# First linear-attention stage of a twelve-stage transformer kernel: every engine in the written order, attention between the other half's feed-forward products, elu without GpSimd, norms in two parts

## The chip, the core and the metric

The kernel runs on one core of a Trainium2 chip. The core has a matrix engine (TensorE, PE in the profile; its weight loads are PEld), VectorE (DVE), ScalarE (ACT), GpSimd (POOL) and a queue engine that issues transfers (SyncE, SP). Each works through its own queue in order and waits on semaphores for the others. Matrix products land in PSUM and have to be copied out ("evacuated") by VectorE or ScalarE before their buffer is free again. The metric is device time in microseconds, the median over several executions; one execution is also recorded by the profiler.

## The reference, cut to what matters

Twelve stages work one after another on a token array of 16 x 64 tokens with 256 features. The change concerns the second, `l0_attn`: four encoder layers with linear attention over blocks of 64 tokens, and a final norm.

```python
qp = elu(q) + 1.0
kp = elu(k) + 1.0
kv = einsum('bshd,bshm->bhmd', kp, v)
z  = 1.0 / (einsum('blhd,bhd->blh', qp, kp.sum(1)) + 1e-6)
attn = einsum('blhd,bhmd,blh->blhm', qp, kv, z)

def layer(x):                       # four times
    h = layernorm(x, ln1)
    q, k, v = h @ Wq + bq, h @ Wk + bk, h @ Wv + bv
    x = x + (attn(q, k, v) @ Wo + bo)
    h = layernorm(x, ln2)
    return x + relu(h @ W1 + b1) @ W2 + b2      # 256 -> 1024 -> 256

y = layernorm(x) * sqrt(256) + position      # before the layers
x = x + layernorm(layers(y)) * lnf_s + lnf_b # after them
```

Beside this the stage computes something for a later one: the sums of squares of 16 x 13 blocks of 128 rows of the long context (`ctx_n`), 208 in all, kept in `self.ss`.

## The kernel before, in words

The 1024 tokens are eight tiles of 128, and the stage treats them as two halves `a` and `b` of four tiles (`Half`, `HT` = 4). One layer of one half has three steps, and I call the three together a half-layer; the stage has eight of them.

- `project` (L462): `norm` (L414) takes the statistics of all four tiles, then one root on ScalarE (inside `rstd`, L112), then scales the four tiles. `transpose` (L135, TensorE and the evacuation at L152) turns them into `hT`. `by_feature` (L428) makes the queries `qT` from `wq`, `by_token` (L437) makes keys and values together from `wkv`. `elu1` (L332) then works on all queries and after that on all keys: GpSimd takes the minimum with zero (L335), ScalarE the exponential (L336), VectorE the maximum and the sum (L337).
- `attend` (L482): for each tile `sums` (products `pk`, masked by VectorE into `kv`, L493) and `apply` (products `po`, divided by VectorE, L506 to L508); then a transpose (evacuated by VectorE L108 and ScalarE L110 in turn) and the product with `wo`, added to the running sum `y` at L523.
- `feed` (L525): a norm, a transpose, eight products with `w1` evacuated in turn by VectorE (L342) and ScalarE (L344), four products with `w2` of eight steps each, added at L523.

`add_row` (L425, GpSimd) adds a bias row to `y` once in `project` and once in `feed`. The generator `context_squares` (L2027) yields one square after another (L2037, ScalarE); `by_feature` and `by_token` draw from it with `squares` after each product. Its transfers (`piece`, 32 of 896 or 768 KB) are issued by SyncE at L2034, into two buffers.

Nothing in this stage is pinned: a scheduler orders the instructions of each engine by the order in which they are written, the dependences and its own idea of costs, and may take later ones earlier. In other stages `self.pinned` is true, and then `mm` and `tr` (L2016, L2022) tell it to keep TensorE's instructions in the order of the text. Weights come by SyncE's queue into rotating buffers (`w2` in `self.wp` eight deep, `w8` three deep), so that a layer's `w1` can only be loaded when the `w1` of the layer before has had its last use. PSUM pools of the stage hold two buffers of each kind.

The order in which the steps are written is: project a, project b, attend a, feed a, attend b; then for each further layer project a, feed b (of the layer before), attend a, project b, feed a, attend b; at the end `end(a)`, feed b, `end(b)`.

Of the kernel before, what the change touches and what calls it, by code (L numbers as in the profile page):

```python
# [11 lines left out]
F32 = mybir.dt.float32  # L12
# [7 lines left out]
P = 128  # L20
# [10 lines left out]
class Streamed:  # L31


    def __init__(self, b):
        self.b = b
# [11 lines left out]
NEVER = -1.5 * 2.0**127  # L47


class Sections:  # L50
# [335 lines left out]
    def l0_attn(self):  # L386
        nc, tc, d = self.nc, self.tc, self.d
        HT = NT // 2
        with ExitStack() as ctx:
            sb = ctx.enter_context(tc.tile_pool(name="l0a", bufs=1))  # L390
            sb2 = ctx.enter_context(tc.tile_pool(name="l0a2", bufs=2))
            ps = ctx.enter_context(tc.tile_pool(name="l0a_ps", bufs=2, space=PSUM))
            pieces = self.context_squares(sb2)
# [5 lines left out]
            mask = self.c("mask136").unsqueeze(1).to_broadcast([P, 2, 136])  # L399
            pos = self.c("pos").unsqueeze(1).to_broadcast([P, HT, D])  # L400

            class Half:


                def __init__(s, i):
                    s.i = i
# [7 lines left out]
            def norm(s, src):  # L414
                mv = sb2.tile([P, HT, 2], F32, tag="ln_mv", name="ln_mv")
                for t in range(HT):
                    st = sb2.tile([P, 6], F32, tag="ln_st", name="ln_st", bufs=3)
                    nc.vector.bn_stats(st, src[:, t, :])
                    nc.vector.bn_aggr(mv[:, t, :], st)
                r = self.rstd(sb2, mv[:, :, 1], 1e-5, "ln_r")  # L420
                for t in range(HT):
                    nc.vector.tensor_scalar(
                        s.n[:, t, :], src[:, t, :], mv[:, t, 0:1], r[:, t : t + 1], ALU.subtract, ALU.mult)

            def add_row(s, r):  # L425
                nc.gpsimd.tensor_tensor(s.y, s.y, r.unsqueeze(1).to_broadcast([P, HT, D]), ALU.add)

            def by_feature(w, xT, evac):  # L428
                for c in range(w.shape[2] // P):
                    pm = ps.tile([P, 512], F32, tag="mm", name="lin_t")  # L430
                    for k in range(KC):
                        nc.tensor.matmul(  # L432
                            pm, w[:, k, c * P : (c + 1) * P], xT[:, k, :], start=(k == 0), stop=(k == KC - 1))
                    evac(c, pm)
                    squares(1)

            def by_token(w, xT, evac):  # L437
                kc, cols = w.shape[1], w.shape[2]
                for t in range(HT):
                    pm = ps.tile([P, cols], F32, tag="mm", name="lin", padded_shape=[P, 512])  # L440
                    for k in range(kc):
                        nc.tensor.matmul(  # L442
                            pm, xT[:, k, t * P : (t + 1) * P], w[:, k, :], start=(k == 0), stop=(k == kc - 1))
                    evac(t, pm)
                    squares(kc // KC)

            def weights(l):
# [10 lines left out]
                for k in ("bq", "b1", "ln1_s", "ln1_b", "ln2_s", "ln2_b"):  # L458
                    setattr(w, k, self.v(f"L0_attn_{k}.{l}"))
                return w  # L460

            def project(s, w):  # L462

                norm(s, s.y)
                self.transpose(ps, s.n, s.hT, w.ln1_s, w.ln1_b)
                add_row(s, w.bo)
                by_feature(w.wq, s.hT, lambda c, pm: nc.scalar.activation(
                    s.qT[:, c, :], pm, AF.Identity, bias=w.bq[:, c : c + 1]))

                def evac_kv(t, pm):  # L470
                    nc.vector.tensor_tensor(s.kz[:, t, :], pm[:, 0:D], w.bk, ALU.add)
                    nc.vector.tensor_tensor(
                        s.va[:, t, :, 0:128], pm[:, D : 2 * D].rearrange("p (g x) -> p g x", g=2),
                        w.bv.rearrange("p (g x) -> p g x", g=2), ALU.add,
                    )

# [1877 lines left out]
```

## Time and profile before

| | us |
|---|---|
| median of 4 runs (lowest, highest) | 3902.28 (3898.74, 3903.39) |
| the profiled execution: its own time | 3905.09 |
| its span, first to last instruction | 3903.3 |
| mean granted TensorE clock in it | 0.958 |

The stage lies between the last addition of the stage before (VectorE, ends at about 875.1 us of the span) and its own last addition (starts 1373.60, takes 1.24). Cut at the starts of the eight feed-forward products with `w2`, busy time of the engines and the granted clock are:

| stretch (us from the span's start) | length | PE | DVE | ACT | POOL | clock |
|---|---|---|---|---|---|---|
| 875.1 to 961.1 | 86.0 | 64.37 | 52.26 | 58.45 | 27.61 | 0.88 |
| 961.1 to 1013.8 | 52.7 | 47.23 | 22.65 | 40.01 | 11.93 | 0.97 |
| 1013.8 to 1072.3 | 58.5 | 53.79 | 28.98 | 17.75 | 11.93 | 0.97 |
| 1072.3 to 1130.7 | 58.4 | 52.29 | 28.97 | 9.96 | 11.93 | 1.00 |
| 1130.7 to 1189.1 | 58.4 | 52.29 | 28.97 | 9.96 | 11.93 | 1.00 |
| 1189.1 to 1247.6 | 58.5 | 52.40 | 28.98 | 9.96 | 11.94 | 1.00 |
| 1247.6 to 1306.0 | 58.4 | 53.69 | 28.99 | 9.95 | 11.94 | 0.97 |
| 1306.0 to 1355.1 | 49.1 | 43.72 | 23.88 | 5.19 | 2.35 | 0.93 |
| 1355.1 to 1374.9 | 19.8 | 13.99 | 8.37 | 0.89 | 0.00 | 0.97 |

A stretch's length less PE is the time in which no product ran at all; products that wait inside a run of their own kind count as busy. All 208 squares run in the first three stretches. A timeline row reads: start, duration, engine, line, operation, output<-inputs, shapes, count; in square brackets stands the idle time before it and what ended it.

### The profile page before, as it was taken

What the parts mean: (1) busy time and instruction counts of PE and PEld (TensorE: products, weight loads), DVE (VectorE), ACT (ScalarE), POOL (GpSimd) and SP (SyncE); (2) the same over time, 40 slices, a digit from 0 to 9 for tenths busy, and PEclk for the clock granted to TensorE, in tenths of its full rate; (3) what the DMA queues carried; (4) which work ended last, traced back from release to release, by engine and by line L of the source; (5) the groups of instructions that cost most, each with busy time, mean ns of one, the idle gap of its engine ahead of it and who ended that gap; (6) DMA issues with size and microseconds to landing.
All of it is one profiled execution on the core that took longest, in us unless ns stands there. A gap on an engine that the chain in (4) does not pass through costs nothing.

```text
span 3903.3 us, 70627 instructions
## 1 busy us (share of the span) xinstructions
PE 3548.6 (91%) x30986; PEld 2245.3 (58%) x30986; DVE 1995.5 (51%) x3623; ACT 1402.4 (36%) x1955; POOL 1339.6 (34%) x767
## 2 busy tenths in 40 slices
PE   8999999978898989999987898899999879999985
PEld 4555555554565555555544566567676655555454
DVE  4333344335454445565657654577777655333346
ACT  2333333336411111444433443266666612111212
POOL 1555555562221101343331100377777730000011
PEclk9999999998999979999998999999999979999987
DMA  3111111005300004323401000211110004111640
GB/s 122 37 37 37 36 37 37 19 31 204 121 28 30 22 19 156 108 91 106 141 25 38 1 6 1 94 50 49 42 54 37 2 10 165 35 41 30 266 172 16
DMA packets 97212, 248.83 MB, mean 64 GB/s; under 512 B 7764, under 2 KB 68831, under 8 KB 94728
## 3 DMA queue, kind: packets, MB, share of 16 engines
q1 hardware_dynamic: 96904, 244.31, 17.6%
q8 instruction: 243, 3.98, 0.4%
q14 instruction: 65, 0.53, 0.0%
HBM read 243.24 MB, written 1.05 MB: 63 GB/s over the span
## 4 chain that ended last, share of the span: by engine, by line
PE 54%; DVE 10%; ACT 3%; issue 2%; POOL 1%; DMA 1%; SPq 0%; DVEq 0%; POOLq 0%; ACTq 0%
PE pk L2018 9%; PE sc L2018 7%; PE lin L177 5%; PE pu L2018 3%; PE acc L2018 3%; PE gate L1619 3%; PE up L1619 3%; PE pc L1246 3%; PE prz L2018 2%; PE lin_t L164 2%; PE lin L442 2%; PE gelu_t L1156 1%; PE turn L2023 1%; PE lin_t L432 1%; PE lin L2018 1%
## 5 line engine op out<-in xcount | busy, mean ns | idle before, releaser
L1957 POOL TENSOR_TENSOR tot<-tot,e 128x1024 f32<-128x1024 f32 (+1 forms) x352 | 831.6, 2362 | 376.0 <-ACT e L304 250.8
L247 DVE TENSOR_REDUCE m<-sc 128x4 f32<-128x2048 f32 x96 | 220.1, 2293 | 270.4 <-PE sc L2018 269.3
L1386 DVE SCALAR_TENSOR_TENSOR e<-sc,row_L_xattn_nbias,free 128x2048 f32<-128x2048 f32 x104 | 244.3, 2349 | 123.5 <-PE sc L2018 116.1
L1388 ACT ACTIVATE e<-e 128x2048 f32<-128x2048 f32 x104 | 198.7, 1910 | 243.3 <-DVE e L1386 243.3
L304 ACT ACTIVATE e<-sc 128x2048 f32<-128x2048 f32 x104 | 195.2, 1877 | 239.8 <-PE sc L2018 239.8
L2018 PE MATMUL sc<-qb,kT 32*128 32x128 f32 x6656 | 245.9, 284 | 38.7 <-DVE m L261 12.4
L2018 PEld LDWEIGHTS sc<-qb,kT 32*128 32x128 f32 x6656 | 206.9, 187 | 84.1 <-issue 24.6
L2018 PE MATMUL acc<-e,v 128*32 128x128 f32 x6656 | 228.1, 278 | 9.1 <-ACT e L1389 9.1
L2018 PEld LDWEIGHTS acc<-e,v 128*32 128x32 f32 x6656 | 171.4, 110 | 110.1 <-issue 96.0
L2018 PE MATMUL pk<-cT,wk 128*128 128x512 f32 (+1 forms) x512 | 207.9, 534 | 3.6 <-DVE rows L277 3.6
L2018 PE MATMUL pk<-wv,cT 128*128 128x256 f32 x832 | 208.6, 392 | 0.0
L1389 ACT ACTIVATE e<-e 128x2048 f32<-128x2048 f32 x104 | 198.8, 1911 | 3.3
L2018 PE MATMUL pk<-cT,wkv 128*128 128x512 f32 (+1 forms) x512 | 196.3, 524 | 0.0
L2018 PE MATMUL pk<-wkv,cT 128*128 128x256 f32 x832 | 196.3, 386 | 0.0
L2018 PEld LDWEIGHTS pk<-wv,cT 128*128 128x128 f32 x832 | 149.2, 189 | 75.3 <-issue 57.2
L2018 PEld LDWEIGHTS pk<-wkv,cT 128*128 128x128 f32 x832 | 153.2, 190 | 28.5 <-issue 4.3
L1246 PE MATMUL pc<-ew,eh 128*128 128x256 f32 x640 | 155.0, 384 | 0.0
L791 POOL TENSOR_TENSOR e<-e,mx 128x512 f32<-128x512 f32 x96 | 81.6, 882 | 212.5 <-DVE mx L790 212.5
L2018 PE MATMUL sc<-kT,qb 32*128 32x512 f32 (+2 forms) x1536 | 139.9, 462 | 13.0 <-issue 1.8
L2018 PE MATMUL pu<-cn,e 128*64 128x257 f32 (+1 forms) x1248 | 143.9, 387 | 5.6 <-POOL e L801 5.6
L1623 ACT ACTIVATE g<-gate 128x512 f32<-128x512 f32 x68 | 40.6, 597 | 295.9 <-PE gate L1619 295.9
L2018 PE MATMUL sc<-cT,qT 128*64 128x512 f32 (+1 forms) x768 | 142.2, 519 | 0.6 <-DVE qT L749 0.5
(476 smaller groups left out, 6389.4 us busy)
## 6 DMA issues: line engine op xcount, KB each, us to landing
cT<-in_ctx_t SPq DMA_DIRECT2D x128, 832.0 KB
cn<-in_ctx_n SPq DMA_DIRECT2D x32, 1664.0 KB
piece<-in_ctx_n SPq DMA_DIRECT2D x16, 896.0 KB
piece<-in_ctx_n SPq DMA_DIRECT2D x16, 768.0 KB
w<-in_L_attn_W SPq DMA_DIRECT2D x8, 1024.0 KB
w<-in_L_ffn_W SPq DMA_DIRECT2D x16, 256.0 KB
down<-in_L_ffn_w_down SPq DMA_DIRECT2D x16, 256.0 KB
gate<-in_L_ffn_w_gate SPq DMA_DIRECT2D x16, 256.0 KB
```

The costliest lines, as they stand in the source:

```text
L164: nc.tensor.matmul(pm, w[:, k, n * P : (n + 1) * P], xT[:, k, h * 512 : (h + 1) * 512], start=(k == 0), stop=(k == kc - 1),)
L177: nc.tensor.matmul(pm, xT[:, k, t * P : (t + 1) * P], w[:, k, :], start=(k == 0), stop=(k == kc - 1))
L247: nc.vector.tensor_reduce(x.m4[:, g, :, i], pm, AX.X, ALU.max)
L304: nc.scalar.activation(e, pm, AF.Exp, scale=0.25)
L791: pin(nc.gpsimd.tensor_tensor(p.e, p.e, p.mx.unsqueeze(2).to_broadcast(p.shape), ALU.subtract))
L1246: nc.tensor.matmul(pc[:, n, j, :], s.eh[i][:, c, tok], ew2[:, c, cols], start=False, stop=(c == 3))
L1386: nc.vector.scalar_tensor_tensor(e16, pm16, nb, free[:, at : at + P].unsqueeze(1).to_broadcast([P, 16, P]), ALU.add, ALU.mult)
L1388: nc.scalar.activation(e, e, AF.Relu)
L1389: nc.scalar.activation(e, e, AF.Square)
L1619: nc.tensor.matmul(pm[-1], w[:, k, n * P : (n + 1) * P], xT[:, k, tok], start=(k == 0), stop=(k == KC - 1))
L1957: nc.gpsimd.tensor_tensor(tot[:w], x.first if c == 1 else tot[:w], e[:w], ALU.add)
L2018: ins = self.nc.tensor.matmul(*args, **kw)
```

## The change

Only `l0_attn`, `context_squares` and a new small class are touched; the instructions of the eleven other stages stand in the same order as before.

- **Written order.** `Written` wraps VectorE, ScalarE and GpSimd so that each of their instructions in the stage is kept in program order; `self.pinned` is set for TensorE.
- **Interleaving.** All steps become generators; `mix` puts the `sums` and `apply` of one half between the `w1` and `w2` products of the other half. The driver below gives the whole order.
- **Norms in two parts.** `measure` takes the statistics and the root of two tiles, `norm` scales them later; `turn` transposes two tiles, VectorE evacuates one half of the result and ScalarE the other (after attention ScalarE all of it).
- **Elu without GpSimd.** The biases are raised by one (`bq1`, `bk1`), the exponential is taken straight from the product in PSUM (queries) or from `kz` (keys), and one VectorE operation makes `max(min(e, 1), z + 1)`.
- **Squares.** The pieces are 48 of 640 or 384 KB, three buffers, loaded two ahead, issued from ScalarE's queue; `feed` alone draws the squares, 28 of them in each of its passes while there are any.
- **PSUM.** Three buffers for the products with weights, two for transposes, one two-bank buffer for `pk`, one for `po`.

```diff
+class Written:
+    def __getattr__(self, name):
+        def issue(*args, **kw):
+            self.tc.keep_in_program_order(getattr(self.engine, name)(*args, **kw))
+        return issue
...
+            def measure(s, src, p):
+                mv = sb2.tile([P, 2, 2], F32, tag=f"ln_mv{s.i}", name="ln_mv")
+                for j in range(2):
+                    st = sb2.tile([P, 6], F32, tag="ln_st", name="ln_st", bufs=3)
+                    V.bn_stats(st, src[:, 2 * p + j, :])
+                    V.bn_aggr(mv[:, j, :], st)
+                r = sb2.tile([P, 2], F32, tag=f"ln_r{s.i}", name="ln_r")
+                V.tensor_scalar(r, mv[:, :, 1], 1.0, 1e-5, ALU.mult, ALU.add)
+                A.activation(r, r, AF.Sqrt)
+                s.by[p] = mv, r
...
+            def turn(s, p, scale=None, shift=None):
...
+                if scale is None:
+                    A.copy(s.hT[:, :, tok], pt.rearrange("p c j x -> p c (j x)"))
+                    return
+                of = [pt[:, c].rearrange("p j x -> p (j x)") for c in range(KC)]
+                V.tensor_scalar(s.hT[:, 0, tok], of[0], scale[:, 0:1], shift[:, 0:1], ALU.mult, ALU.add)
+                A.activation(s.hT[:, 1, tok], of[1], AF.Identity, bias=shift[:, 1:2], scale=scale[:, 1:2])
...
             def project(s, w):
-                t2 = s.tmp.rearrange("p t x -> p (t x)")
-                for z in (s.qT.rearrange("p c x -> p (c x)"), s.kz.rearrange("p t x -> p (t x)")):
-                    self.elu1(z, t2, z)
...
+                turn(s, 0, w.ln1_s, w.ln1_b)
+                yield
+                for t in range(2):
+                    kv(t)
+                    yield
+                turn(s, 1, w.ln1_s, w.ln1_b)
+                add_row(s, w.bo)
+                exp_keys(0)
+                yield
+                for c in range(KC):
+                    pm = by_feature(w.wq, c, s.hT)
+                    A.activation(qe[c], pm, AF.Exp, bias=w.bq[:, c : c + 1])
+                    A.activation(s.qT[:, c, :], pm, AF.Identity, bias=w.bq1[:, c : c + 1])
+                    larger(*(two(0) if c == 0 else (s.qT[:, 0, :], qe[0])))
+                    yield
+                kv(2)
+                larger(s.qT[:, 1, :], qe[1])
+                yield
+                kv(3)
+                yield
+                exp_keys(2)
+                larger(*two(2))
...
             def attend(s, w):
                 for t in range(HT):
+                    sums(t)
+                    yield
+                    if t:
+                        apply(t - 1)
+                        yield
+                apply(HT - 1)
+                turn(s, 0)
+                yield
+                turn(s, 1)
+                yield
+                for t in range(HT):
+                    pm = by_token(w.wo, t, s.hT)
+                    V.tensor_tensor(s.y[:, t, :], pm, s.y[:, t, :], ALU.add)
+                    if t % 2:
+                        measure(s, s.y, t // 2)
+                    yield
+                    if t % 2:
+                        norm(s, s.y, t // 2)
+                        yield
...
+            def feed(s, w, last=False):
...
+                for c in range(8):
...
+                    squares(1 + c % 2)
+                    yield
+                for t in range(HT):
+                    pm = by_token(w.w2, t, s.h1T)
+                    V.tensor_tensor(s.y[:, t, :], pm, s.y[:, t, :], ALU.add)
+                    if t % 2:
+                        measure(s, s.y, t // 2)
+                    elif t:
+                        finish(s, 0, last)
+                    squares(4)
+                    yield
+                finish(s, 1, last)
...
+            def mix(at, fd):
+                for f, t in ((5, 1), (1, 1), (1, 2), (1, 2), (1, 1), (1, 0), (1, 1), (1, 1)):
+                    go(fd, f)
+                    go(at, t)
+                go(fd)
+                go(at, 5)
...
             for l in range(1, 4):
                 w0, w = w, weights(l)
-                project(a, w)
-                feed(b, w0)
-                attend(a, w)
-                project(b, w)
-                feed(a, w)
-                attend(b, w)
+                for s, ws, o, wo in ((a, w, b, w0), (b, w, a, w)):
+                    mix(at, fd)
+                    fd2 = feed(o, wo, l == 3 and o is a)
+                    pr = project(s, ws)
+                    go(pr, 1)
+                    go(at)
+                    at, fd = attend(s, ws), fd2
+                    go(pr, 6)
+                    go(fd, 1)
+                    go(pr, 1)
+                    go(fd, 1)
+                    go(pr)
+            mix(at, fd)
+            go(at)
+            go(feed(b, w, True))
+            squares(999)
...
-    def context_squares(self, pool):
+    def context_squares(self, pool, act):
+        todo = [(b, lo, min(lo + 5, NCH)) for b in range(B) for lo in range(0, NCH, 5)]
+        loaded = []
+        for i, (b, lo, hi) in enumerate(todo):
+            while len(loaded) < min(i + 3, len(todo)):
...
+                act.dma_start(piece[:, : hi2 - lo2, :], rows[:, lo2:hi2, :])
```

`go(it, n)` runs a generator for n of its yields, so that `go(pr, 6)` is six steps of `project`. Before the loop the driver runs: the first norms of `a`, `project(a)` with the first norms of `b` between its products, `project(b)` with the `sums` and `apply` of `a` between its products, then `attend(a)` to its end and the two transposes of `feed(a)`. The last two norms (`lnf`) are done inside `finish` for two tiles at a time, and the row `lnf_b` is now written at the start (GpSimd; before it was written in `end`, L536, and ran at 880.23).

More of the change, by code (lines that the diff above doesn't have):

```diff
@@ L425, in add_row @@
-            def add_row(s, r):
[L426 to L435, printed above, removed]
@@ L467, in project @@
[L467 to L475, printed above, removed]
```

228 lines of the change are left out of this document (140 added, 88 removed).

## The prediction, before the result was known

> **What bounds the kernel now.** First the page, for the whole program:
>
> ```profile
> span 3903.3 us, 70627 instructions
> ...
> PE 54%; DVE 10%; ACT 3%; issue 2%; POOL 1%; DMA 1%; SPq 0%; DVEq 0%; POOLq 0%; ACTq 0%
> ```
>
> TensorE carries most of the chain that ended last, so a gain has to come from time in which TensorE stands still. The change touches only the stage from 875.1 to 1374.86 us (499.8). There I read TensorE's timeline over one half-layer, and beside it those of ScalarE and GpSimd:
>
> ```profile
> 1189.14 13.98 PE L442 MATMUL lin<-w,h1T 128*128 128x256 f32 x64
> 1203.05 0.74 PE L490 MATMUL pk<-va,kz 64*128 64x136 f32 x8
> 1204.31 0.73 PE L490 MATMUL pk<-va,kz 64*128 64x136 f32 x4 [0.52 <-DVE kv L493]
> ...
> 1206.61 0.74 PE L490 MATMUL pk<-va,kz 64*128 64x136 f32 x8
> 1207.28 0.68 PE L501 MATMUL po<-kv,qT 128*64 128x136 f32 x8
> 1207.90 1.38 PE L490 MATMUL pk<-va,kz 64*128 64x136 f32 x8
> ...
> 1213.21 2.76 PE L442 MATMUL lin<-wo,hT 128*128 128x256 f32 x12
> 1215.81 1.04 PE L143 MATMUL tr<-cst,n 128*128 128x128 f32 x8
> 1217.95 3.70 PE L432 MATMUL lin_t<-hT,wq 128*128 128x512 f32 x8 [1.11 <-DVE hT L152]
> 1221.49 7.03 PE L442 MATMUL lin<-wkv,hT 128*128 128x512 f32 x16
> 1228.35 1.04 PE L143 MATMUL tr<-cst,n 128*128 128x128 f32 x8
> 1232.08 3.70 PE L432 MATMUL lin_t<-hT,w 128*128 128x512 f32 x8 [2.69 <-DVE hT L152]
> 1237.18 10.57 PE L432 MATMUL lin_t<-hT,w 128*128 128x512 f32 x24 [1.40 <-DVE h1T L342]
> 1247.59 2.75 PE L442 MATMUL lin<-w,h1T 128*128 128x256 f32 x12
> ```
>
> The period is 1247.59 - 1189.14 = 58.45. The work in it, from start to next start: w2 13.91, w1 10.41 for 24 so 13.88 for 32, wkv 6.86, wq 3.54, wo 2.60 for 12 so 3.47, pk 4 x 0.67, po 4 x 0.62, three transposes of about 1.0: **49.8**. So 8.6 us of each half-layer are lost: 6.0 in brackets (with one of 0.30 not shown), the rest inside runs (the third pk run takes 1.38 where another takes 0.74). The two largest stand behind the elu:
>
> ```profile
> 1227.03 1.06 ACT L336 ACTIVATE tmp<-tmp 128x1024 f32<-128x1024 f32 x1 [3.29 <-POOL tmp L335]
> 1234.15 1.06 ACT L336 ACTIVATE tmp<-tmp 128x1024 f32<-128x1024 f32 x1 [6.07 <-POOL tmp L335]
> ```
>
> GpSimd takes 3.62 us for each minimum; VectorE's two long elu operations then delay the evacuations that TensorE needs.
>
> The stage's opening is worse, and cold:
>
> ```profile
> 884.50 1.99 PE L143 MATMUL tr<-cst,n 128*128 128x128 f32 x8 [9.77 <-DVE n L422]
> 887.17 6.30 PE L432 MATMUL lin_t<-hT,wq 128*128 128x512 f32 x8 [0.69 <-DVE hT L152]
> ...
> 1336.92 1.99 PE L143 MATMUL tr<-cst,n 128*128 128x128 f32 x8 [3.52 <-DVE n L422]
> ```
>
> After these idle times the same eight transposes take 1.99, not 1.04, and wq's 8 take 6.15, not 3.54; the granted clock is 0.50 there.
>
> **The change, step by step.** I follow the written order and add up. Durations: VectorE's evacuations 0.42 (128x256) and 0.75 (128x512), statistics of a tile 0.34 + 0.1, root 0.20, the squares:
>
> ```profile
> L2037 ACT ACTIVATE junk<-piece 128x256 bf16<-128x256 f32 x208 | 83.3, 403 | 16.1 <-DMA piece<-in_ctx_n 16.1
> ```
>
> (0.40 for each; the last entry is idle time before them that ended with a transfer's landing).
>
> *A steady half-layer* begins with w1's first product at 0. The pk and po of the other half lie between w1 and w2 products; a w1 product takes 1.74, VectorE needs 0.8 for a tile's masks, 0.75 for a division, 0.75 for every second relu, and keeps up; the 0.52, the 1.38 and their like go. GpSimd's two minima (7.24) leave the path; in their place ScalarE takes 0.65 per exponential and VectorE 0.65 per maximum (half of L337's 1.23 for 128x1024). Four waits of TensorE appear:
>
> 1. *wo's third tile, 2.3.* The second transpose of attention is now copied by ScalarE alone, and in its queue stand before it a root and four squares. After the last w2 product: addition and statistics on VectorE 1.65, root 0.25, four squares 4 x 0.40, one transfer issue 0.35, copy 0.59 (L234's 128x512): 4.45. TensorE has a transpose and two wo tiles meanwhile: 0.5 + 2 x 0.87 = 2.2. Behind the squares stand the copy, the next roots and so the next norm.
> 2. *the first wkv, 1.6.* After wo's last tile: addition, statistics, VectorE's evacuation 2.1, less a transpose of 0.5.
> 3. *wq, 0.8*: VectorE evacuates two wkv halves (0.75) before the second transpose.
> 4. *w1, 0.8*: the same after the last wkv tile.
>
> Sum 49.8 + 5.5 = **55.3**, against 58.45: 3.1 gained. There are six such half-layers.
>
> An issue on ScalarE does not occur before. SyncE's rows for the same transfer have 0.33; lower bound 0, upper 2.02 (its longest of a weight here, with its wait inside). I take 0.35, as most rows say; one issue a half-layer lies on the path, so the upper end costs 7 x 1.7 = 12. Whether pieces land in time: an issue at 874.75 was used at 880.23, 5.5 later, at full load; two pieces ahead are 8 or more squares, and between the bursts of squares ScalarE idles some 8 us. So nothing, except for the very first piece: ScalarE waits 5 us there, three product buffers absorb all but 0.9.
>
> *Opening.* From 875.1, VectorE has statistics 2.1, two norms with their statistics 5.0, a norm 0.9; the first transpose at 883.1, evacuated at 884.7. Two wkv tiles at cold speed (0.77 for each of 4, as wq shows): 890.7. VectorE then has b's statistics before the evacuation (893.0); wq, wq, wkv to 898.3; ScalarE has to change tables exp, root, exp, root, exp at 1.28 each, so buffers and b's norms come late: b's first transpose is evacuated only at 908.2. Two cold wkv 5.3, transpose and evacuation: 914.8. Then 17.2 of work for pk, wq, po, wkv, transposes and wo to 932, a norm 2.7, transposes and evacuation 1.1: w1 at 935.8, **60.7** after the stage's start. The squares (58 us of ScalarE's time in the old opening's 86) are gone from here.
>
> *Closing*, from w1 of the last feed of a: 35.6 work + 2.3 + 1.75 = 39.6; norm and evacuation 3.7; w1 13.9 and 1.9 for the cold start (15.68 at 1339.60 shows it); w2 13.9; then two tiles' addition, statistics, norm, scaling: 4.2, where the old tail of four tiles took 5.74. **77.2**.
>
> The stage: 60.7 + 0.9 + 6 x 55.3 + 77.2 = 470.6 against 499.8: **29.2 less**. Cover that this uses: GpSimd's rows (2.36 each) and the roots stay beside products; if VectorE fell behind by 1 us a half-layer in the interleaved part, that would cost 7.
>
> The weights' queue: SyncE loses the 32 pieces (0.33 each, and their waits for squares), so that nothing is later; a layer's w1 load still waits for the old w1's last product, 38 us before its next use.
>
> The row says of a table change 1.28 us, and the root that follows one starts at 877.52 after a load that began at 876.23: no more than the load. [...]
>
> **Rivals.**
> - *The new waits take all that the old ones gave* (ScalarE's squares and transfers before every copy): the half-layer stays at 58.45. For it: four waits stand where five stood. Against: the elu's 2.69 and 1.40 have no successor of their size. Gain 29.2 - 6 x 3.1 = 10.6: 3892.
> - *Nearly only TensorE's work is left*, because squares slip into ScalarE's idle time and the copy is not late: half-layer 51.5, gain 29.2 + 6 x 3.8 = 52: 3850. Against: the squares are written before the copy.
> - *Slower: ScalarE's queue is held by the pieces.* It now issues and awaits them in order, and relu, copies and exponentials stand behind. For it: 16.1 us of such waits before, with larger buffers. If each feed waited once for a whole landing of 5.5: 7 x 5.5 = 38.5, 9.3 slower: 3912. It decides from 4.2 us a feed. Against: the long idle stretches before each burst.
> - *The scheduler had already done it*, so that the written order changes nothing: the brackets above show that it had not.
>
> **The numbers.** The profiled execution took 3905.09 (span 3903.3), the median is 3902.28; the difference is taken from the median: 3902.28 - 29.2 = **3873**. Chances: forecast 0.63 (3863 to 3884: a microsecond and a half more or less in each half-layer), first rival 0.17, second 0.13, slower 0.07. The range 3852 to 3893 takes in the second rival's nearer part, the first, and the issue's upper bound (3885). Within 0.2% (7.8 us) is about what a measurement can't tell from no change: 0.04, out of the first rival; faster 0.89; slower 0.07.
>
> **What would show it.** The period between w2's first products should be about 55; no idle before w1 over 1 us; 2 us before wo's third tile that end with ScalarE's copy; the squares spread over the stage; the first w1 about 61 us into it. I am wrong if ScalarE shows idle time ended by pieces of more than a few us, if VectorE ends waits between w1 products, or if the opening is no shorter.

## The result, and the profile after

| | before | after |
|---|---|---|
| median (lowest to highest), us | 3903.78 (3889.99 to 3913.88), 64 runs | 3911.84 (3898.83 to 3919.34), 44 runs |
| ratio after / before | | 1.0017, 95% interval 1.0011 to 1.0022 |
| profiled execution: span, mean granted clock | 3903.3, 0.958 | 3898.1, 0.957 |
| the stage in it | 499.8 | 506.2 |

The change made the kernel 0.17% slower; a gain of 29.2 us was forecast. The profiled execution of after happens to lie below its own median. In the seventeen other profiles of this study the time outside the stage lies between 3395 and 3409 us, in this one at 3392, though its instructions there are in the same order. So the stage is read by itself; the 6.4 by which it grew agree with the ratio (0.0017 x 3904 = 6.6).

The page, span and chain of waits by engine:

```profile
span 3898.1 us, 70720 instructions
...
PE 75%; DVE 13%; ACT 7%; issue 2%; POOL 1%; DMA 1%; ACTq 0%; DVEq 0%; POOLq 0%; SPq 0%
```

These shares are of the whole program, of which the stage is an eighth, so they do not settle it. Cut in three at the first `w1` product of the first and of the last feed, the windows of after (the columns are those of the table before: length, then busy time of PE, PEld, DVE, ACT and POOL with counts, then the clock):

```profile
874.20:944.30 70.10, 41.66 (x160) 21.41 (x160) 46.27 (x139) 22.52 (x36) 13.01 (x8) 0.81 0.11 37
944.30:1298.90 354.60, 317.54 (x1345) 194.58 (x1345) 169.94 (x479) 147.05 (x467) 32.87 (x19) 0.97 0.29 92
1298.90:1380.40 81.50, 70.82 (x288) 45.41 (x288) 36.38 (x99) 27.78 (x101) 2.35 (x1) 0.94 0.22 70
```

GpSimd went from 101.6 us in the stage to 48.2, as meant. But the opening takes 70.1 where 61.6 were forecast, the six half-layers 354.6 (59.1 each) where 331.8 were, the closing 81.5 where 77.2 were: 8.5 + 22.8 + 4.3 = 35.6, the whole error.

TensorE's timeline, where one half's feed meets the other half's attention and the next projection (called the junction below), then the next such place:

```profile
980.88 1.89 PE L2165 MATMUL lin<-wo,hT 128*128 128x256 f32 x8
985.23 3.56 PE L2165 MATMUL lin<-wo,hT 128*128 128x256 f32 x8 [2.45 <-ACT hT L58]
988.58 0.76 PE L2170 MATMUL tr<-cst,n 128*128 128x128 f32 x4
991.03 3.70 PE L2165 MATMUL lin<-wkv,hT 128*128 128x512 f32 x8 [1.69 <-DVE hT L58]
...
996.03 3.70 PE L2165 MATMUL lin_t<-hT,wq 128*128 128x512 f32 x8 [0.86 <-DVE hT L58]
...
1043.92 1.99 PE L2165 MATMUL lin<-wo,hT 128*128 128x256 f32 x8 [2.28 <-ACT hT L58]
```

The four waits stand where they were forecast and have nearly the forecast size: 2.45 before wo's third tile, 1.69 before wkv, 0.86 before wq, 0.95 before w1 (not shown). What was not forecast is the duration 3.56: eight such products take 1.89 one line above and 1.99 in the next half-layer. The windows over the 3.56 and over the 1.99 give granted clocks (the number after the five busy times) of 0.54 and 1.00:

```profile
985.20:988.60 3.40, 3.38 (x9) 2.57 (x10) 2.08 (x6) 0.20 (x1) 0.86 (x1) 0.54 0.22 88
...
1043.90:1045.80 1.90, 1.88 (x9) 1.63 (x10) 1.53 (x6) 0.20 (x1) 1.02 (x1) 1.00 0.66 236
```

Five of the six half-layers have such a run, in wo or in wkv (5.40 instead of 3.70), at a granted clock of 0.53 to 0.68, and take 58.9 to 60.7 us; the one without takes 57.53.

### The profile page after: what moved, and what is told of

The parts are those of the page before. It is cut to its first block, busy times and chain, and to the rows that moved or that the text cites. A ratio compares the mean times of both kernels' runs of the same rounds, so it can differ in the third digit from the quotient of the medians.

```text
span 3898.1 us, 70720 instructions
## 1 busy us (share of the span) xinstructions
PE 3534.3 (91%) x30986; PEld 2227.3 (57%) x30986; DVE 1994.6 (51%) x3637; ACT 1438.0 (37%) x2027; POOL 1287.1 (33%) x760
## 4 chain that ended last, share of the span: by engine, by line
PE 75%; DVE 13%; ACT 7%; issue 2%; POOL 1%; DMA 1%; ACTq 0%; DVEq 0%; POOLq 0%; SPq 0%
PE pk L2165 14%; PE sc L2165 14%; PE lin L2165 6%; PE acc L2165 5%; PE lin L189 5%; PE lin_t L2165 5%; ACT e L316 4%; PE pu L2165 3%; PE gate L1766 3%; PE up L1766 3%; PE pc L1393 3%; PE prz L2165 2%; PE lin_t L176 2%; PE gelu_t L1303 2%; PE turn L2170 1%
```

## The experiments

All ratios are to the kernel before, timed on the same chip. "Opening" is the first w1 product counted from the stage's start, "half-layer" the time between first w1 products.

| label | edit | ratio (95%) | stage | opening | half-layers |
|---|---|---|---|---|---|
| after | | 1.0017 (1.0011 to 1.0022) | 506.2 | 70.1 | 57.5 to 60.7 |
| e1 | last squares drawn earlier | 1.0030 (1.0017 to 1.0042) | 512.5 | 70.0 | 59.2 to 62.3 |
| e2 | next transposes ahead of wo | 0.9971 (0.9959 to 0.9984) | 489.6 | 70.3 | 55.6 to 58.3 |
| e3 | five products added | 1.0019 (1.0006 to 1.0032) | 506.5 | 72.6 | 58.8 to 58.9 |
| e4 | before, with the new elu alone | 0.9922 (0.9904 to 0.9939) | 466.1 | 63.4 | 54.4 |
| e6 | after, V, A and G in free order | 0.9930 (0.9911 to 0.9949) | 473.0 | 60.2 | 54.7 to 57.7 |
| e7 | attention behind the feed | 1.0114 (1.0098 to 1.0130) | 547.6 | 70.2 | 63.6 to 67.2 |
| e9 | wkv among the wo tiles | 1.0007 (0.9995 to 1.0018) | 499.5 | 70.1 | 57.7 to 58.4 |
| e10 | e9 and e1 | 0.9989 (0.9978 to 1.0000) | 494.5 | 69.0 | 55.7 to 60.6 |
| e11 | e1, e2's transposes, norms late | 1.0021 (1.0011 to 1.0031) | 510.3 | 70.2 | 58.7 to 60.3 |
| e13 | opening alone in free order | 0.9989 (0.9978 to 1.0000) | 493.9 | 58.0 | 57.5 to 60.7 |
| e14 | e11 and e13 | 0.9995 (0.9985 to 1.0006) | 497.5 | 57.7 | 58.6 to 60.3 |
| e8 | no exponential in layer 0 (its elu is left out) | 1.0009 (0.9997 to 1.0021) | 503.1 | 67.1 | as after |
| e15 | norms late, mended | 0.9919 (0.9900 to 0.9939) | 472.9 | 70.3 | 53.3, first 55.2 |
| e16 | e15 and e13 | 0.9901 (0.9886 to 0.9916) | 462.2 | 59.3 | 53.3, first 55.4 |
| e12 | e15, V, A and G in free order | 0.9903 (0.9885 to 0.9921) | 462.6 | 59.2 | 52.7 to 53.0, first two 55.3 and 55.9 |
| e17 | two products added | 0.9984 (0.9974 to 0.9994) | 501.0 | 69.2 | 57.5 to 62.1 |

V, A and G are VectorE, ScalarE and GpSimd.

### First four: the squares, the wkv wait, the clock, the elu

```diff
-                    squares(4)
+                    squares((6, 6, 4, 0)[t])
```

> The changed kernel, with the four squares that follow a feed's last w2 tile drawn two tiles earlier (6, 6, 4 and 0 behind the four tiles instead of 4 each); nothing else. Theory (the squares stand ahead of ScalarE's copy, and the wait they make, close to the next one, lets TensorE's clock fall): the chain to the copy is then addition and statistics 1.65, root 0.25, copy 0.59, against 2.2 of TensorE's work, so the wait before wo's third tile falls from 2.45 us to about 0.4, and the slow wo or wkv runs (3.6 instead of 2.0) are gone: 6 x 2.0 + 5 x 1.65 = 20 less in the stage, 506 to about 486, ratio to the kernel before about 0.9965. Rival 1 (the copy is late for another reason, or the wait only moves to the next place): stage 506, ratio 1.002. Rival 2 (the wait goes, the slow clock stays because one wait of 2 us is enough for it): 12 less, 494, ratio 0.9985.

The first wait went, as expected, and the time came back a few lines on. TensorE in this kernel:

```profile
982.83 1.99 PE L2165 MATMUL lin<-wo,hT 128*128 128x256 f32 x8 [0.34 <-ACT hT L58]
984.66 0.60 PE L2170 MATMUL tr<-cst,n 128*128 128x128 f32 x4
989.45 6.66 PE L2165 MATMUL lin<-wkv,hT 128*128 128x512 f32 x8 [4.19 <-DVE hT L58]
```

0.34 + 4.19 = 4.53 is as much as the two waits are in after's half-layer at full clock (2.28 + 2.25), nearly in one piece, and a longer slow run follows (wkv 6.66 instead of 3.70). Rival 1 was right: the two waits are one wait, for something that ends later than both. VectorE's timeline in after shows what:

```profile
980.64 0.43 DVE L58 TENSOR_TENSOR y<-lin,y 128x256 f32<-128x256 f32 x1 [2.56 <-PE lin L2165]
...
982.82 0.73 DVE L58 TENSOR_SCALAR n<-y,ln_mv,ln_r 128x256 f32<-128x256 f32 x2
983.47 0.75 DVE L58 TENSOR_TENSOR y<-lin,y 128x256 f32<-128x256 f32 x2
...
986.55 0.74 DVE L58 TENSOR_SCALAR n<-y,ln_mv,ln_r 128x256 f32<-128x256 f32 x2
987.21 0.42 DVE L58 TENSOR_TENSOR y<-lin,y 128x256 f32<-128x256 f32 x1
988.82 0.42 DVE L58 TENSOR_TENSOR y<-lin,y 128x256 f32<-128x256 f32 x1 [1.20 <-PE lin L2165]
...
990.44 0.54 DVE L58 TENSOR_SCALAR hT<-tr,vecs 128x256 f32<-128x256 f32 x1
```

From the feed's last addition at 980.64, VectorE does that tile's statistics and norm, then four additions, statistics and a norm of attention, and only then, at 990.44, the evacuation of transposes whose operand (the feed's first norm) had been ready before 980. TensorE has 4.5 us of work meanwhile (wo 3.5, two transposes). In e1, with no wait of ScalarE's in between, the chain from the addition to the evacuation still takes 980.36 to 988.86.

```diff
                 go(fd)
-                go(at, 5)
+                go(at, 3)
+                go(pr, 1)
+                go(at, 2)
```

> The changed kernel, with the first transposes of the next projection (4 products, their norm was ready long before) issued ahead of attention's last two wo tiles instead of after them. Theory: the first wkv then has its operand when wo ends, so the wait of 1.7 to 2.6 us before it goes; 0.5 us of the wait before wo's third tile is filled by the transposes (2.45 to about 1.9); with one wait instead of two the clock stays up (1.65 in 5 half-layers): 6 x (2.0 + 0.5) + 8 = 23 less in the stage, 506 to about 483, ratio about 0.996. Rival 1 (VectorE's evacuation of the transposes now stands before the addition that the norm needs, and the wait comes back before w1): stage 495 or more, ratio at least 0.999. Rival 2 (the slow clock comes from the wait before wo alone): 15 less, 491, ratio 0.998.

Transposes and evacuation now stand ahead of wo's last two tiles in both queues. TensorE:

```profile
1042.99 1.99 PE L2166 MATMUL lin<-wo,hT 128*128 128x256 f32 x8 [1.84 <-ACT hT L58]
1045.74 3.70 PE L2166 MATMUL lin<-wkv,hT 128*128 128x512 f32 x8 [0.75 <-DVE hT L58]
```

The wait before wkv falls to 1.10 at most, in three half-layers to nothing, and the stage to 489.6: 17 less of the 23 expected. wo was still slow in the first and the third half-layer (3.51 and 2.94 for 1.99), each time after a single wait of 2.02, though not in the fourth after the same wait (1.99): one wait of 2 us can be enough for that; rival 2, with its 491, was the nearest.

> The changed kernel, with work added: five products of 128x512 (0.44 each, 2.2 together, result unused) on TensorE ahead of wo's third tile in every attention, where TensorE waits 2.45. Theory (the second half of the loss is TensorE's clock, which falls because two waits of 2 us stand close together): the added work lies in the wait, the clock stays up, and the slow wo or wkv runs (3.6 for eight products instead of 2.0) are gone: 5 x 1.65 = 8 less in the stage, 506 to 498, ratio about 0.9998, though 15 us of work were added. Rival (the runs are long because they wait inside for operands, not for the clock): the runs stay long, stage 506 to 508, ratio 1.002 or more.

The five products took 4.46 us and not 2.2: the rows count each twice (x10), and so 2.1 too much was added to every half-layer. Even so the half-layers take 58.85, none over 58.9: wo takes 1.89 and wkv 3.70, after a wait of 1.81, and the granted clock is 1.00 from 1063 to 1300 us. The clock part was right; the amount was not. The stage of 506.5 is the rival's number, but not for the rival's reason:

```profile
983.57 4.46 PE L2169 MATMUL fill<-qT,cst 128*128 128x512 f32 x10
987.86 1.89 PE L2169 MATMUL lin<-wo,hT 128*128 128x256 f32 x8
...
991.99 3.70 PE L2169 MATMUL lin<-wkv,hT 128*128 128x512 f32 x8 [1.81 <-DVE hT L58]
```

The fourth goes from the other side: the kernel before with the new elu alone.

```diff
-                for z in (s.qT.rearrange("p c x -> p (c x)"), s.kz.rearrange("p t x -> p (t x)")):
-                    self.elu1(z, t2, z)
+                for t in (0, 2):
+                    z, e = (a[:, t : t + 2, :].rearrange("p t x -> p (t x)") for a in (s.kz, s.tmp))
+                    nc.scalar.activation(e, z, AF.Exp, bias=less)
+                    nc.vector.scalar_tensor_tensor(z, e, 1.0, z, ALU.min, ALU.max)
```

> The kernel before, with the new elu alone (biases plus one, the exponential from the product on ScalarE, minimum and maximum on VectorE, none on GpSimd); order, attention, norms and pieces as before. Theory (the elu was worth what was reckoned, 2.69 + 1.40 of waits before w1 in each half-layer, and the loss of the change is in its order): 6 x 3 to 4 = 18 to 24 less, and some 5 in the opening: stage 499.8 to about 475, ratio about 0.994. Rival (GpSimd's minima were hidden or VectorE's share of the elu takes their place): stage 495 to 500, ratio 0.999 to 1.0.

It did better than expected: 33.7 less in the stage, 4.1 in each half-layer (54.36 between runs of pk). TensorE:

```profile
1190.12 3.70 PE L432 MATMUL lin_t<-hT,wq 128*128 128x512 f32 x8 [1.10 <-DVE hT L152]
...
1201.95 13.90 PE L432 MATMUL lin_t<-hT,w 128*128 128x512 f32 x32
```

The waits of 2.69 and 1.40 before and in w1 are gone. So the elu alone is worth more than the whole change was forecast to be, and the rest of the change (order, interleaving, two-part norms, pieces) costs 506.2 - 466.1 = 40 us.

### Order or interleaving

e6 takes `keep_in_program_order` away from the three engines and leaves it to TensorE; e7 issues attention whole behind the feed (`go(fd)`, then `go(at, 14)` in `mix`).

> The changed kernel, with the written order kept for TensorE alone: VectorE, ScalarE and GpSimd are put in order by the scheduler again. Theory (VectorE's queue: between the last w2 product and the first wkv product TensorE has 4.4 us of work, VectorE has 8.5 us in a row, and the evacuation that wkv needs stands last in it): a scheduler that draws this evacuation forward gains the 2 us before wkv, and stage 506 becomes 485 to 495, ratio 0.995 to 0.998. Rival (it is TensorE's own order, attention drawn in between w1 products, that takes the cover away, and no order on VectorE brings it back): the waits at the junction stay near 4 in sum, stage 503 to 508, ratio about 1.001.

> The changed kernel, with the attention of the other half issued whole after the feed's last w2 product, as in the kernel before, instead of between its w1 and w2 products; all else, the written order too, as changed. Theory (the interleaving took from the junction the 5.3 us of pk and po products that had covered VectorE's statistics and norms): wo's third tile waits less, the waits between pk and po come back (0.5 to 1 each, 3 to 5 a half-layer), the switches between w1 and pk (1.4) go: half-layer 54 to 57, stage 475 to 495, ratio 0.994 to 0.998. Rival (the written order on VectorE and ScalarE costs as such, wherever attention stands): the pk and po waits come on top, half-layer 61 or more, stage 515 or more, ratio 1.004 or more.

e6: 33 of the 40 us are this written order of VectorE, ScalarE and GpSimd. TensorE's order was not touched, so the rival (TensorE's order itself) falls. The opening takes 60.2, the later half-layers 54.8, both close to the forecast. Of the junction's waits the one before wo is gone and one of about 2.0 before wkv is left:

```profile
1135.98 3.62 PE L2165 MATMUL lin<-wo,hT 128*128 128x256 f32 x16
...
1142.05 3.70 PE L2165 MATMUL lin<-wkv,hT 128*128 128x512 f32 x8 [2.01 <-DVE hT L58]
```

e7: my reading that attention behind the feed would cover VectorE's norms was wrong, 547.6 instead of 475 to 495; the rival (515 or more) was right. In written order VectorE finishes the feed's norm before the first masks, and TensorE waits for these:

```profile
1108.78 0.76 PE L2162 MATMUL pk<-va,kz 64*128 64x136 f32 x8 [3.14 <-DVE kv L58]
...
1126.38 5.40 PE L2162 MATMUL lin<-wkv,hT 128*128 128x512 f32 x8 [3.23 <-DVE hT L58]
```

and the wkv wait is there as well. So the interleaving is worth some 41 us to this written order (547.6 - 506.2; by the ratios 38); without it the same idea is much slower.

### Mending the junction by hand

e9 draws the first wkv tiles in among the wo tiles, e10 adds e1's edit to it.

> The changed kernel, with the first part of the next projection issued among attention's wo tiles: first transposes right after the feed's last w2 tile, then wo, wo, the first wkv tile (1.74 of TensorE's work, ready since the norm of the first two tiles), wo, the second wkv tile, wo. Theory (VectorE's 8.5 us against TensorE's 4.4 at the junction; TensorE's work that depends on nothing in that chain was issued behind it): 3.5 us of work are moved into the waits, so that of 4.1 (2.45 + 1.7 to 2.6) less than 1.5 is left, and the clock stays up: 6 x 3 + 8 = 26 less in the stage, 506 to about 480, ratio about 0.9945. Rival 1 (VectorE itself is the bound of the whole half-layer, so the wait comes back before w1 or wq): stage 490 or more, ratio 0.998 or more.

> The same, and also the squares of the last w2 tile drawn two tiles earlier (6, 6, 4, 0), which alone gained nothing because VectorE's chain took the place of ScalarE's. Theory: with the chain covered the squares are again what the copy before wo's third tile waits for, so that this edit now gains up to 0.5 to 1 a half-layer over the kernel that differs by it alone: 3 to 6 less, stage about 475, ratio about 0.993. Rival (the squares never were on the path): the same time as without them, within 2.

e9: wo and wkv lose their long waits, but wq now waits 3.02 for VectorE's second evacuation, which stands behind the same chain:

```profile
1050.62 5.40 PE L2168 MATMUL lin_t<-hT,wq 128*128 128x512 f32 x8 [3.02 <-DVE hT L58]
```

Rival 1 was right again in where the wait comes back; its reason, VectorE's amount of work, falls with e15 below. e10 is 5 below e9 in the stage, as its theory said, but the intervals of the two ratios overlap.

e11 therefore takes work out of VectorE's chain: attention's statistics and norms, needed only by the feed's transposes, go behind the projection's evacuations (the diff below shows this part). It also has e1's order of the squares and, as in e2, the projection's first transposes ahead of wo.

```diff
-                    if t % 2:
+                    if t % 2 and not late:
                         measure(s, s.y, t // 2)
...
+                if late:
+                    for step in (measure, norm):
+                        for p in range(2):
+                            step(s, s.y, p)
+                            yield
```

> The changed kernel, all in written order, with three places of that order altered at the junction between a feed's last w2 product and the next w1: the projection's first transposes before attention's wo tiles, attention's statistics and norms on VectorE behind the projection's evacuations (they are needed only by the feed's transposes, some 12 us later), and no squares behind the last w2 tile. Theory (the lost time is the place of VectorE's and ScalarE's work in the written order, not its amount): before wo's third tile some 0.3 is left, before wkv nothing, wq and w1 keep 0.86 and 0.95, the clock stays up: 51.2 + 2.1 = 53.3 a half-layer, stage 506 - 6 x 5.7 = 472, ratio about 0.992. Rival (VectorE's amount of work bounds the junction, so the wait reappears before wq or w1): half-layer 56 or more, stage 490 or more, ratio at least 0.997.

From wo to wq it did what was expected (0.15, nothing, 1.08), and all of it came back behind that, 0.86 before the last wkv tiles and 3.74 before w1:

```profile
1183.33 10.52 PE L2172 MATMUL lin_t<-hT,w 128*128 128x512 f32 x20 [3.74 <-ACT hT L58]
```

Two faults of this kernel's own order are in its rows. On ScalarE a root now stood behind the keys' exponential, so that tables were loaded twice more ahead of q; and VectorE's operation on q ran while GpSimd added a row:

```profile
1173.05 1.28 ACT L58 ACT_TABLE_LOAD   x1
1174.35 0.20 ACT L58 ACTIVATE ln_r<-ln_r 128x2 f32<-128x2 f32 x1
1174.56 1.28 ACT L58 ACT_TABLE_LOAD   x1
```

```profile
1179.27 2.39 DVE L58 SCALAR_TENSOR_TENSOR qT<-h1T,qT 128x512 f32<-128x512 f32 x1
```

```profile
1178.77 2.35 POOL L58 TENSOR_TENSOR y<-y,row_L_attn_bk.2_8271 128x1024 f32<-128x1024 f32 x1 [12.73 <-DVE n L58]
```

e15 is meant to mend both: the two `measure` steps go ahead of the exponentials, and `add_row(s, w.b2)` moves from the feed's second transposes to its second w1 product.

> The kernel with the norms late, mended in the two places where the time came back before w1 (3.74): both roots now stand on ScalarE ahead of the exponentials, so that no table is loaded twice, and GpSimd's row (2.35, in which one VectorE operation of 0.69 took 2.39) is moved from before w1 to w1's second product. Theory (only the place of the work in the written order counts): wo's third tile 0.2, wkv nothing, wq 1.1 to 1.4, w1 0.95, clock up: 51.2 + 2.5 = 53.7 a half-layer, stage 506 - 6 x 5.3 = 474, ratio about 0.9935. Rival (VectorE's amount of work bounds the junction and the wait comes back at another place once more): half-layer 57 or more, stage 495 or more, ratio 0.999 or more.

```profile
1145.60 1.13 PE L2173 MATMUL lin<-wo,hT 128*128 128x256 f32 x4 [0.15 <-DVE y L58]
1146.57 3.60 PE L2173 MATMUL lin<-wkv,hT 128*128 128x512 f32 x8
...
1151.69 3.70 PE L2173 MATMUL lin_t<-hT,wq 128*128 128x512 f32 x8 [1.09 <-DVE hT L58]
...
1160.61 8.82 PE L2173 MATMUL lin_t<-hT,w 128*128 128x512 f32 x20 [0.91 <-issue]
```

51.2 + 0.15 + 1.09 + 0.91 = 53.35, and the half-layers take 53.27 to 53.31, with the clock at 1.00 (from 1063 to 1300 us), in all but the first (55.2, whose first w1 products take 10.67 instead of 8.82). The amount of work on VectorE is that of after (28.9 busy in a half-layer; 28.4 there). This settles the junction: the loss was the place of the work in the queues.

Of the two repairs only the first is seen to act. GpSimd's addition starts 0.09 after VectorE's last norm in e15 as in e11, wherever it was written, and it meets a VectorE operation again, now the one on the keys, for which TensorE does not wait here:

```profile
1153.41 2.36 POOL L58 TENSOR_TENSOR y<-y,row_L_attn_bk.2_8270 128x1024 f32<-128x1024 f32 x1 [4.89 <-DVE n L58]
```

```profile
1154.30 2.02 DVE L58 SCALAR_TENSOR_TENSOR kz<-tmp,kz 128x512 f32<-128x512 f32 x1 [0.98 <-ACT tmp L58]
```

The addition comes earlier because the norm does, and the norm does because no root stands behind an exponential any more. The two edits were not tried apart.

### The opening

> The changed kernel, with VectorE, ScalarE and GpSimd put in order by the scheduler in the opening alone (up to the first feed), and in written order after it. Theory (the loss has two separate places): the first w1 comes some 60 us after the stage's start instead of 70, as with all of the order free, and the half-layers stay at 58 to 61: 10 less, stage 496, ratio about 0.999. Rival (the opening's gain is lost again in the first half-layer, whose clock and waits depend on it): stage 503 or more, ratio 1.001 or more.

> Both together: the junction's order altered, and the opening's order free. Theory (the two add up): 34 + 10 less than the changed kernel, stage about 462, ratio about 0.990, which is faster than the kernel before with the new elu alone (0.992). Rival (they overlap): as the better one of the two alone, within 3 us.

> The changed kernel, with the identity in place of the exponential in the first layer (the elu of layer 0 is left out so far, the output is another), which takes five of the six loads of tables out of the opening; all else as changed. Theory (the opening is longer by VectorE's order, of which ScalarE's loads are a part: VectorE waits 3.2 us for ScalarE's q at 898.3, and b's norm stands behind it): 3 to 4 less, first w1 66 to 67 us after the stage's start instead of 70. [...] Rival 2 (the loads lie wholly beside other work): no change, 70.

e13: the opening falls by 12.1 to 58.0 and the half-layers stay as they were; the two losses are separate. The largest part lies at b's first transposes, 33.7 after the stage's start in after and 26.9 in e13; first after, then e13:

```profile
907.88 1.23 PE L2170 MATMUL tr<-cst,n 128*128 128x128 f32 x4 [4.32 <-DVE n L58]
```

```profile
898.83 0.60 PE L2174 MATMUL tr<-cst,n 128*128 128x128 f32 x4
```

e14 shows the same on top of e11 (12.8 off its stage); its own theory of 462 fell with e11. e8 took six loads of 1.28 out (seven in after's opening, one in its own; five were expected) and its opening is 3.0 shorter, as VectorE's idle time in after had suggested; the two ratios overlap:

```profile
901.56 0.69 DVE L58 SCALAR_TENSOR_TENSOR qT<-h1T,qT 128x512 f32<-128x512 f32 x1 [3.19 <-ACT qT L58]
```

The 3.0 is not shown to be a part of the 12: e13 gains 12.1 with every exponential of the first layer in place. The 12 is the order, in which b's norms wait on VectorE behind operations of a's projection whose operand is late. That it is VectorE's order, and not ScalarE's or GpSimd's, is read from the rows; the three were freed together.

> The same, with VectorE, ScalarE and GpSimd put in order by the scheduler in the opening alone. Theory (opening and junction add up; the opening alone was worth 12 in the stage): stage about 462, ratio about 0.990, faster than the kernel before with the new elu alone. Rival (they overlap): no more than the better of the two.

> The same instructions in TensorE's order as there, but VectorE, ScalarE and GpSimd put in order by the scheduler throughout. Theory: the scheduler places the squares and norms at least as well as the order written by hand: half-layer 53 to 54, opening 60, stage 460 to 466, ratio 0.990 to 0.991. Rival (with TensorE's order fixed it draws the statistics ahead of the evacuations again, as with the changed kernel's order, where 2.0 was left before wkv): half-layer 54.8, stage 472, ratio 0.993.

Both came as expected: 462.2 and 462.6, 38 us faster than the kernel before. e16 has the lowest ratio here (3867.51 against 3904.61 beside it). Against the new elu alone it is some 8 lower by the ratios (0.9901 and 0.9922, whose intervals overlap) and 3.9 by the stages (462.2 and 466.1): that it is faster is not shown, and nearly all of the gain is the elu's. With these edits the scheduler's order and the one written by hand do equally well.

### The clock, with less filling

> The changed kernel, with two products of 128x512 added ahead of wo's third tile in every attention (five took 4.46 us, so two take 1.8, less than the wait of 2.45), result unused. Theory (the slow runs after the two close waits are TensorE's clock): the wait hides the added work, the clock stays at full speed, wo and wkv take 1.89 and 3.70: half-layers about 57.5 instead of 58.9 to 59.3, 5 x 1.65 = 8 less, stage 498, ratio about 0.9997, below the changed kernel although work was added. Rival (the clock does not depend on it, or 0.65 of wait is enough to lower it): 58.9 and more, ratio 1.0017 or more.

Ratio 0.9984 against 1.0017 for after, intervals apart: 1.9 us of products were added to each attention for nothing, and the kernel became, by the ratios, some 13 us faster than after. The stages of the two profiles differ by 5.2 (501.0 and 506.2); where the rest is, they do not show. In its profile four of the six half-layers take 57.5, in after's one does. TensorE, in the first half-layer and the second:

```profile
987.40 5.40 PE L2169 MATMUL lin<-wkv,hT 128*128 128x512 f32 x8 [2.08 <-DVE hT L58]
...
1046.67 3.70 PE L2169 MATMUL lin<-wkv,hT 128*128 128x512 f32 x8 [2.25 <-DVE hT L58]
```

The clock in the two is 0.67 and 1.00. After two waits of about the same length it falls once and once not. How often it does in other executions of a kernel, one profile cannot tell.

## Why the prediction was wrong, point by point

- **Elu: right, and too small.** 2.69 and 1.40 of waits were named as what GpSimd's minima cost; without them a half-layer loses 4.1 (e4), and the opening gains too.
- **The four waits: right in place and nearly in size.** 2.3 + 1.6 + 0.8 + 0.8 = 5.5 was forecast, 6.0 to 6.4 came (6.2 on average). The reason given for the first was half of it: the squares are late, but behind them stands VectorE's chain, so that taking them away gains nothing (e1). That the waits are one wait was not seen, because wo's and wkv's were each worked out alone, with the other assumed.
- **The step that failed in the half-layer: "work 49.8" at full clock.** It was added up from one half-layer of the kernel before, with the clock at 1.00 and the products of a kind in long runs. Of the 3.8 that each half-layer is over 55.3, the lowered clock takes 1.7 on average (1.6 to 1.7 in five of six, and the first begins with w1 products at 10.63 for 8.82), the waits' excess 0.7, and the remaining 1.4 is the work itself: 57.53 less 6.30 of waits is 51.2 in the half-layer at full clock. A run of four w1 products takes 1.92 between pk and po instead of 1.74, and from start to start all of w1 takes 14.5 for 13.88, w2 14.2 for 13.91, wo 3.7 for 3.47; that it is this switching that makes the 1.4 was not tried alone. The record of before already had the falling clock: after the same wait of 2.69 it fell in two of five half-layers (0.91 over w1 at 1056.76, 1.00 at 1115.20). There it cost nothing, because a wait of 1.40 inside w1 took it up: from w1's first product to w2's it is 15.51 in both.

```profile
1056.76 15.67 PE L432 MATMUL lin_t<-hT,w 128*128 128x512 f32 x32 [2.69 <-DVE hT L152]
...
1115.20 3.70 PE L432 MATMUL lin_t<-hT,w 128*128 128x512 f32 x8 [2.69 <-DVE hT L152]
1120.30 10.57 PE L432 MATMUL lin_t<-hT,w 128*128 128x512 f32 x24 [1.40 <-DVE h1T L342]
```

- **The step that failed in the opening: "I follow the written order and add up".** The sum followed one chain of durations and left out most of the time in which VectorE stands still in written order, such as the 3.19 us in which it waits for q. It falls behind step by step: the first wkv came 12.5 us into the stage and not 9.6, b's first evacuation at 37.1 and not 33.1, the end of wo at 64.1 and not 56.9, the first w1 at 70.1 and not 60.7. Counted like this the kernel before has its first w1 at 72.2, so the opening became 2.1 shorter. With the three engines in free order (e6) the opening takes 60.2, the six half-layers 333.6, the closing 79.3: 473.0 in all, 2.4 from the 470.6 of the forecast. The forecast was near what a free order gives, but in the half-layers partly by luck: e6's later ones have 3.8 of waits instead of 5.5, and 1.2 more work.
- **The closing**: 81.5 for 77.2. The wait before wo's third tile is 3.03 there instead of 2.3, the norm and evacuations from the last wo product to the last w1 take 5.1 instead of 3.7, and the last w1 run takes 16.50 instead of 15.8; the rest was not broken down.
- **Transfers on ScalarE's queue: right.** An issue takes 0.33 or 0.34 (three in a row 1.36 together); there is one wait for a piece of 3.7 us, at the first.
- **The rivals.** "The new waits take all that the old ones gave" is what happened in the half-layer (59.1 for its 58.45), but its 3892 took the opening's gain as sure. The rival on the slow side was the wrong one: it put the danger into transfers, and the order itself was it; that its 3912 is what was measured (3911.84) is an accident. "The scheduler had already done it" was set aside because of the waits of 2.69 and 1.40. Those were the elu's: with the new elu alone (e4) the scheduler's order has half-layers of 54.36, less than the 55.3 forecast for the written one.
- **The table loads.** The row's reading held: six loads of 1.28 fewer (e8), 7.7 together, gained 3.0 in the opening. Part of them lies beside other work, and in after a root or an exponential whose operand is there starts 0.01 to 0.02 after its load, so no run shows a load that takes more than its 1.28.

## What to carry to other kernels

Before rewriting an order, try the smaller change by itself under the scheduler's order: here the elu alone gave 33.7 of the 37.6 us that the best order reached. Writing an engine's order out by hand freezes every place in it: go through the queue of the busiest helper engine from each TensorE wait backwards, and move behind the evacuation whatever is not needed by then. A wait that ends with another engine when it is removed has only shown the second chain of the same length; look for what both are waiting for before counting the first as gain. Where TensorE waits about 2 us between products, read the granted clock of the products behind as well: here it was 0.53 to 0.68 behind some such waits, and the lower clock took 1.7 us a half-layer on average.

## What the runs showed of the hardware

**The clock was lower after some short waits.** In after, five waits of 2.08 to 2.61 us were followed by products at a granted clock of 0.53 to 0.68 (wo 3.56 at 0.54 after 2.45, wkv 5.40 at 0.68 after 2.08), and others by products at 1.00 (wo 1.99 after 2.28, in another half-layer after 2.45 and in the closing after 3.03; wkv 3.70 after 2.25). After the waits of 1.81 in e3 wkv took 3.70, with the clock at 1.00 from 1063 to 1300 us. In e9 wq took 3.70 after a wait of 3.02 in the first half-layer and 5.40 after the same wait in the second; there, and in e1 and e2, the clock is judged by such durations alone. What decides is not shown: in the first three half-layers of after, e8 and e13, whose order is the same from the first feed on, wo was slow in the first and the third and not in the second (3.56, 1.99, 3.63 in after and e8; 3.68, 1.99, 3.51 in e13), though their feeds begin at 944.3, 942.5 and 929.9 us of their spans.

**Some VectorE operations were longer beside a GpSimd addition.** In e11 an operation with two inputs in SBUF, 0.69 in after, took 2.39: begun 0.50 after GpSimd's addition, it ended 0.54 after it (1181.66 and 1181.12). In e15 another took 2.02 instead of 0.69 and ended 0.55 after the addition. An operation of 128x2 with one input in SBUF took 0.75 instead of 0.17 beside such an addition (at 985.34 in after, ended 0.03 after it). Additions from PSUM ran at 0.41 to 0.42 beside such a row (e11, at 1178.60 and 1178.93). Why is not shown.
